# A graph-attention kernel: the next batch's load placed behind the store that frees its tile, its split and one batch's pieces reordered

## The chip, the cores and the metric

The kernel runs on one core of a Trainium2 chip. The core has a matrix engine (TensorE, in the profile PE, with PEld for its weight loads), three engines for element work (VectorE or DVE, ScalarE or ACT, GpSimd or POOL) and SyncE (SP), which here only starts transfers. The metric is the device time of one execution in microseconds, as the median of several runs. Before the change it is 4039.82 us (three runs, 4035.16 to 4045.39).

## The reference

The input x has 32 batches of 512 nodes with 512 features. Two layers follow each other, both with a residual and a normalisation over the features:

```python
# layer 0: messages along the graph
mi = einsum('bkd,od->bko', x, Wi)
mj = einsum('bkd,od->bko', x, Wj)
a = adj.astype(x.dtype)
deg = a.sum(axis=1)
out = deg[None, :, None] * (mi + b) + einsum('ij,bjo->bio', a, mj)
x = layernorm(x + out)
# layer 1: attention over the graph's edges, 8 heads of 64
q, k, v = x @ Wq.T + bq, x @ Wk.T + bk, x @ Wv.T + bv      # split in heads
scores = where(adj == 0, -inf, q @ k.T / 8)
x = layernorm(x + softmax(scores) @ v @ Wo.T + bo)
```

All batches use the same weights and the same adjacency matrix, and no batch depends on another.

## The kernel before, in words

**Pipeline over batches.** The work of the 32 batches is laid out in periods. In period n (`for n in range(1, B + 1)`, the loop around L695) TensorE does the attention of batch b = n - 1 in 8 steps: scores (L427), the product with the values (L448), the sums of the softmax (L455). Between these it does the dense products of three batches: `phase_b(n)` has layer 0 of batch n together with the output projection of m = n - 2; `phase_c(n)` has the v, q and k products of batch n; `phase_a(n + 1)` has the "gather" of batch n + 1 and what is left of k. Each phase returns a list of pieces in a fixed order with an estimated cost each (`PC, TR, GA = 1.73, 0.44, 1.9` us); `by_steps` cuts the list into 8 shares. The engines then run their instructions in just the order in which this list emits them: there is no scheduler behind it. An item of cost 0 (`z(...)`) is emitted where it stands.

**Pieces.** A product of 512x512 by 512x512 is cut into 2x2 blocks and done with seven block products instead of eight, numbered 1 to 7 and done in the order 1, 2, 6, 7, 4, 5, 3 (`ORDER`). `piece` (L359) does one of them: eight records of matmuls in a v, q, k or projection piece, sixteen in a layer 0 piece, since that has two products. Results are gathered in two PSUM banks, `mma` and `mmb`. Products 6, 7 and 4 add up in one bank, 5 and 3 in another (`GROUP`), so after 6 or 7 VectorE must have read the bank before the next of the group may go on in it.

**The gather of a batch.** `l0_gather` (L283) treats one quarter of x's features: four transposes on TensorE ("turning", L292), a product with the degrees on VectorE (L293), and eight matmuls with the adjacency matrix (L299) that use x split in a high and a low part. `split` (L178) makes these: ACT copies the high part `xhi` (L183), GpSimd subtracts to get the low part `xlo` (L184). `ahead` (L187) makes the first two of a batch's four splits; the others follow inside the gather.

**Tiles of x and their transfers.** A batch's x is 1 MB. There are three tiles for it, named `xh` (L106), and x is worked on in place until the batch is stored (L477). In period n, batch m = n - 2 is stored in `phase_c(n)`, right after its final normalisation (ACT, L272), and its tile takes x of batch n + 1 (`load_x`, L107), which the gather wants at the end of the same period. So a load must wait for the end of a store. SyncE starts all transfers in the order of the program, and it also starts the loads of the weight blocks: `prefetch` (L250) puts a new one into a ring of 12 tiles (L253) after each piece, when its TensorE work has freed one. An instruction of SyncE that waits holds back all that stand behind it.

**What the change touches.** In `phase_c`, the last items are the pairs of q and v pieces for products 6, 7, 4, 5, 3 (L600 to L603); `load_x(n + 1)` stands behind the pair of product 5 (L604, L605), and `ahead(n + 1)` behind all of them (L606, L607). In `phase_b`, the first period with n = 1 has no batch m yet, and its layer 0 pieces have an order of their own (L558), followed by the statistics of the first rows behind piece 4, the normalisation (`apply`), and two turnings of the normalised rows (`l0_norm`, L320).

Of the kernel before, what the change touches and what calls it, by code (L numbers as in the profile page):

```python
# [25 lines left out]
def gnn_attention_kernel(  # L26
# [35 lines left out]
    B, N, D = x.shape  # L62
# [266 lines left out]
    def quarter(src, j, n):  # L329
        return src[:, 2 * j:2 * j + 2, Q * n:Q * n + Q]  # L330
# [153 lines left out]
    def z(f, *a):  # L484
        return (0.0, f, *a)

    def pc(kind, b, i, bank):
        return (2 * PC if kind == "l0" else PC, piece, kind, b, i, bank)
# [4 lines left out]
    def banks(n):  # L493

        return ("a", "b") if n % 2 == 0 else ("b", "a")
# [46 lines left out]
    def project(m, i):  # L542

        res = [pc("pj", m, i, banks(m)[1])]
        if i == 1:
            res = [z(combos, TO, m, ot_quarter(m), (1,))] + res
        if i == 2:
            res = [FLUSH] + res + [z(combos, TO, m, ot_quarter(m), (2, 3, 4))]
        return res

    def phase_b(n):

        m = n - 2
        if m < 0:
            res = []
            side = [z(add_bo, 0, i) for i in range(2)]
            A, K = banks(n)
            for i, bank in ((2, A), (6, K), (5, A), (7, K), (3, A), (4, K)):  # L558
                res.append(pc("l0", n, i, bank))
                if i == 4:  # L560
                    res += [z(stats, n, 0)]
                res += side[:1]
                side = side[1:]
            return res + [z(apply, n, 0), z(stats, n, 1), (TR, l0_norm, n, 0), (TR, l0_norm, n, 1)]
        res = project(m, 1)
        for i in ORDER[1:]:
            res.append(pc("l0", n, i, banks(n)[0]))
            if i == 4:
                res.append(z(stats, n, 0))
            if i == 5:  # L570
                res.append(z(stats, m, 0))
            if i == 3:
                res += [z(stats, n, 1), (TR, l0_norm, n, 1)]
            res += project(m, i)
            if i == 4:
                res.append(z(apply, n, 0))
            if i == 5:
                res.append((TR, l0_norm, n, 0))
            if i in (7, 4):
                res.append(z(add_bo, n - 1, int(i == 4)))  # L580
        return res

    def phase_c(n):

        m = n - 2
        norm = [(TR, l0_norm, n, ic) for ic in range(NC)]
        h = lambda j, i: quarter(HT[n], j, i)
        A, K = banks(n)
        res = [pc("v", n, 1, A)] + ([z(apply, n, 1)] if n else []) + [pc("q", n, 1, K)]
        if m >= 0:  # L590
            res += [z(stats, m, 1)]
        res += [pc("v", n, 2, A), norm[2], norm[3], z(combos, TH, n, h, (1, 2)), pc("k", n, 1, A),
                z(combos, TH, n, h, (3, 4)), pc("q", n, 2, K), pc("k", n, 2, A)]
        side = []
        if n == 0:

            side = [z(graph_forms, 2), None, z(graph_forms, 0), None, z(graph_forms, 1)]
        if m >= 0:
            res += [z(apply, m, 0), z(apply, m, 1), z(store, m)]
        for i in ORDER[2:]:  # L600
            for f in pc("q", n, i, K), pc("v", n, i, A):
                res += [f] + [g for g in side[:1] if g]
                side = side[1:]  # L603
            if i == 5 and n + 1 < B:  # L604
                res += [z(load_x, n + 1)] if n > 0 else []  # L605
        if n + 1 < B:  # L606
            res += [z(ahead, n + 1)]  # L607
        return res

    def fold(part):  # L610
# [59 lines left out]
    def flags():  # L670
# [5 lines left out]
        nc.vector.tensor_scalar(again, tot, -1.0, 1.0, op0=OP.mult, op1=OP.add)  # L676

    PERIODS = [first() + phase_c(0) + phase_a(1)]
    PERIODS += [by_steps(phase_b(n) + phase_c(n) + phase_a(n + 1)) for n in range(1, B)]
    PERIODS += [last_steps()]  # L680
    for f in PERIODS[0] + [f for p in PERIODS[1:] for todo in p for f in todo]:
# [191 lines left out]
```

## Time and profile before

| what | value |
|---|---|
| time, median of 3 | 4039.82 us |
| span of the profiled execution | 4048.5 us |
| TensorE busy | 3902.1 us, 96% |
| VectorE / GpSimd / ScalarE busy | 2595.3 / 1862.8 / 1058.3 us |
| mean granted TensorE clock | 0.986 of full speed |
| loads of x, 1 MB each: start to landing | median 5.7 us |
| stores of x, 1 MB each: start to landing | median 5.2 us |

Three kinds of views are used. The table of waits gives, for an engine and a line, what it waited for: microseconds in total, times, longest. The timeline lists instructions with their start, their duration, engine and line, and in brackets how long the engine had been idle and what ended the idle time. A table of windows gives, for a stretch of the execution, each engine's busy time and number of instructions, and then the granted clock, the share of DMA and GB/s. A wait is put down to what came last; idle time of an engine that isn't the bottleneck costs nothing.

### The profile page before, as it was taken

How to read it: one execution, taken by the hardware profiler on the slowest of the kernel's cores; microseconds unless marked ns; L12 is line 12 of the kernel's file. 1: busy time of each engine (PE TensorE's matmuls, PEld its weight loads, DVE VectorE, ACT ScalarE, POOL GpSimd, SP SyncE). 2: the span in 40 equal slices, each digit the busy share in tenths (PEclk: the TensorE clock that was granted, in tenths of full speed). 3: DMA queues.
4: the chain of work that ended last, by engine and by line, in shares of the span. 5: the costliest groups of instructions: out<-in, count | busy, mean ns of one | idle time of the engine just before them, and what ended most of it. 6: DMA issues, size and time to landing. Idle time of an engine off the chain costs nothing.

```text
span 4048.5 us, 46895 instructions
## 1 busy us (share of the span) xinstructions
PE 3902.1 (96%) x17370; PEld 2663.9 (66%) x17370; DVE 2595.3 (64%) x3525; ACT 1058.3 (26%) x1476; POOL 1862.8 (46%) x1861
## 2 busy tenths in 40 slices
PE   9999999999999999999999999999999999999997
PEld 6666666666666666666666666666666666666663
DVE  4566665666666666666666666666666666666666
ACT  2222222222222222222223222222222222222322
POOL 4355444454434544345444445443454434544433
PEclk9999999999999999999999999999999999999998
DMA  7333333333334233333333433333423333333330
GB/s 247 107 104 97 110 99 115 107 98 104 110 106 123 84 112 102 108 117 92 104 110 104 117 105 100 103 107 110 122 81 111 106 110 114 104 97 110 102 110 22
DMA packets 281866, 433.86 MB, mean 107 GB/s; under 512 B 23073, under 2 KB 119841, under 8 KB 281633
## 3 DMA queue, kind: packets, MB, share of 16 engines
q1 hardware_dynamic: 281376, 430.27, 35.3%
q8 instruction: 141, 2.31, 0.2%
q14 instruction: 93, 0.75, 0.1%
q0 software_dynamic: 256, 0.53, 0.0%
HBM read 389.29 MB, written 41.42 MB: 106 GB/s over the span
## 4 chain that ended last, share of the span: by engine, by line
PE 72%; DVE 11%; POOL 9%; DMA 4%; issue 2%; ACT 1%; SPq 0%; POOLq 0%
PE mma L375 20%; PE mmb L375 20%; PE sc L427 10%; PE ov L448 9%; POOL xh L390 5%; DMA xh<-in_x_dram 4%; PE mmb L299 3%; PE mma L299 3%; DVE rl L461 3%; PE ov L455 2%; DVE st L265 2%; DVE xh L393 2%; POOL big L344 2%; DVE e L432 2%; POOL es L438 2%
## 5 line engine op out<-in xcount | busy, mean ns | idle before, releaser
L432 DVE TENSOR_TENSOR e<-sc,edge 128x1024 f32<-128x1024 f32 x512 | 602.4, 1218 | 467.3 <-ACT sc L431 467.3
L431 ACT ACTIVATE sc<-sc 128x1024 f32<-128x1024 f32 x512 | 492.9, 1007 | 1279.8 <-PE sc L427 1279.3
L375 PE MATMUL mmb<-ring,big 128*128 128x256 f32 x3144 | 734.6, 382 | 7.9 <-POOL big L344 7.9
L375 PE MATMUL mma<-ring,big 128*128 128x256 f32 x3112 | 724.2, 381 | 3.1 <-POOL big L344 2.9
L375 PEld LDWEIGHTS mmb<-ring,big 128*128 128x128 f32 x3144 | 593.2, 191 | 131.4 <-DVE e L432 23.5
L375 PEld LDWEIGHTS mma<-ring,big 128*128 128x128 f32 x3112 | 584.7, 190 | 125.4 <-DVE e L432 25.2
L344 POOL TENSOR_TENSOR big<-big 128x512 f32<-128x512 f32 x376 | 549.7, 1488 | 222.3 <-DVE big L293 177.9
L184 POOL TENSOR_TENSOR xlo<-xh,xhi 128x512 fp32r<-128x512 f32 x128 | 163.4, 1287 | 911.6 <-ACT xhi L183 909.4
L427 PE MATMUL sc<-q,k 64*128 64x512 f32 x2048 | 513.8, 620 | 0.0
L448 PE MATMUL ov<-e,v 128*64 128x512 f32 x2048 | 497.8, 607 | 8.2 <-DVE oT L471 8.2
L461 DVE RECIPROCAL rl<-ov 128x128 f32<-128x128 f32 x512 | 462.4, 929 | 5.6 <-PE ov L455 1.8
L375 PE MATMUL mma<-big,ring 128*128 128x256 f32 x1808 | 433.1, 382 | 2.2 <-DVE xh L393 2.2
L375 PE MATMUL mmb<-big,ring 128*128 128x256 f32 x1776 | 425.3, 382 | 3.2 <-DVE xh L393 2.4
L267 POOL TENSOR_SCALAR mv<-mv 128x1 f32<-128x1 f32 x256 | 50.3, 196 | 747.2 <-DVE mv L266 737.1
L375 PEld LDWEIGHTS mma<-big,ring 128*128 128x128 f32 x1808 | 337.9, 190 | 80.5 <-issue 26.0
L375 PEld LDWEIGHTS mmb<-big,ring 128*128 128x128 f32 x1776 | 332.2, 190 | 78.7 <-issue 24.3
L438 POOL TENSOR_TENSOR es<-e 128x1024 f32<-128x1024 f32 x128 | 300.7, 2349 | 176.5 <-PE ov L455 176.5
L448 PEld LDWEIGHTS ov<-e,v 128*64 128x64 f32 x2048 | 124.8, 136 | 349.0 <-issue 275.3
L440 DVE TENSOR_TENSOR es<-es,e 128x1024 f32<-128x1024 f32 x256 | 339.6, 1327 | 0.1
L427 PEld LDWEIGHTS sc<-q,k 64*128 64x128 f32 x2048 | 178.8, 189 | 214.4 <-issue 212.2
L393 DVE TENSOR_TENSOR xh<-xh,mmb 128x512 f32<-128x512 f32 x186 | 125.7, 676 | 217.4 <-PE mmb L375 216.4
L390 POOL TENSOR_TENSOR xh<-xh,p 128x512 f32<-128x512 f32 x186 | 231.7, 1274 | 72.4 <-ACT sc L431 39.0
(141 smaller groups left out, 3746.1 us busy)
## 6 DMA issues: line engine op xcount, KB each, us to landing
ring<-wq SPq DMA_DIRECT2D x160, 256.0 KB, 2.6
ring<-wv SPq DMA_DIRECT2D x160, 256.0 KB, 2.7
ring<-wk SPq DMA_DIRECT2D x160, 256.0 KB, 3.8
ring<-wi SPq DMA_DIRECT2D x155, 256.0 KB, 2.7
ring<-wj SPq DMA_DIRECT2D x155, 256.0 KB, 2.7
ring<-wo SPq DMA_DIRECT2D x155, 256.0 KB, 2.6
xh<-in_x_dram SPq DMA_DIRECT2D x32, 1024.0 KB, 5.7
out_dram<-xh SPq DMA_DIRECT2D x31, 1024.0 KB, 5.2
```

The source lines that it names most:

```text
L299: nc.tensor.matmul(pm, parts[w][:, jc, :], adjR[:, jc, :], start=(w == 0 and jc == 0), stop=(w == 1 and jc == NC - 1))
L344: nc.gpsimd.tensor_tensor(dst, p, q, op=OP.subtract)
L375: nc.tensor.matmul(pm[:, c * Q:(c + 1) * Q], lhs, rhs, start=first, stop=(kc == 1 and n == len(terms) - 1), skip_group_check=True)
L390: nc.gpsimd.tensor_tensor(d, d, p1, op=OP.add)
L393: nc.vector.tensor_tensor(d, d, pm, op=OP.add)
L427: nc.tensor.matmul(ps[:, s, :], KT[b, hp // 2][r, hp % 2, kc * P:(kc + 1) * P], QT[b, hp // 2][r, hp % 2, :], start=True, stop=True)
L431: nc.scalar.activation(ps, ps, AF.Exp, scale=QSCALE)
L432: nc.vector.tensor_tensor(e, ps, edge[:, kc:kc + 1, :].to_broadcast([P, 2, N]), op=OP.mult)
L438: nc.gpsimd.tensor_add(ES[hp], E[0], E[1])
L440: nc.vector.tensor_add(ES[hp], ES[hp], E[half])
L448: nc.tensor.matmul(PV[hp][s * HD:(s + 1) * HD, :], V[b][:, kc, c0:c0 + HD], E[kc][:, s, :], start=(kc == 0), stop=(kc == NC - 1))
L461: nc.vector.reciprocal(rl[:, c], pl[:, c])
```

## The change

Three edits of the order of the program; no instruction is added or taken away.

1. `load_x(n + 1)` moves from behind the q and v pieces of product 5 to behind those of product 7, four pieces earlier. The store of batch n - 2 stands ahead of the pieces of product 6, so the load comes close behind the store whose tile it takes.
2. `ahead(n + 1)`, the first two splits, moves from behind the pieces of product 3 to behind those of product 5, two pieces ahead of the turning.
3. In period 1, layer 0's piece 4 comes ahead of piece 3. The statistics of the first rows, which are emitted behind piece 4, come earlier with it.

The aim is that x of the next batch, and its split, are there when TensorE comes to turn it, and that in period 1 the normalised rows are there when TensorE turns them.

```diff
@@ phase_b(n), the period without a batch m
-            for i, bank in ((2, A), (6, K), (5, A), (7, K), (3, A), (4, K)):
+            for i, bank in ((2, A), (6, K), (5, A), (7, K), (4, K), (3, A)):
                 res.append(pc("l0", n, i, bank))
                 if i == 4:
                     res += [z(stats, n, 0)]
@@ phase_c(n)
             for f in pc("q", n, i, K), pc("v", n, i, A):
                 res += [f] + [g for g in side[:1] if g]
                 side = side[1:]
+            if i == 7 and 0 < n < B - 1:
+                res += [z(load_x, n + 1)]
             if i == 5 and n + 1 < B:
-                res += [z(load_x, n + 1)] if n > 0 else []
-        if n + 1 < B:
-            res += [z(ahead, n + 1)]
+                res += [z(ahead, n + 1)]
         return res
```

## The prediction

> **What bounds the kernel now.** I read the page's busy table first, then the waits of TensorE, then the timeline of one period, then windows with the granted clock. The busy table says which engine to look at:
>
> ```profile
> PE 3902.1 (96%) x17370; PEld 2663.9 (66%) x17370; DVE 2595.3 (64%) x3525; ACT 1058.3 (26%) x1476; POOL 1862.8 (46%) x1861
> ```
>
> TensorE (PE) is busy in 3902.1 of 4048.5 us; no other engine is over 64%. So only two things can shorten the run: less idle on PE (146.4 us), or faster matmuls. The waits of PE (total us, times, longest) say who owns the idle:
>
> ```profile
> PE sc L292 <- DMA xh<-in_x_dram: 89.3, 30, 5.5
> PE ov L448 <- DVE oT L471: 8.2, 4, 3.0
> PE mmb L375 <- POOL big L344: 7.9, 15, 5.0
> PE sc L320 <- ACT xh L272: 3.2, 2, 2.9
> ```
>
> One wait, 30 times, owns 89.3 us: the turning of the next x (L292) waits for the load of that x. Every other is under a tenth of it. The fourth line matters for the third edit. One period, from the store of an old batch to the scores behind the first gather, then the second gather for comparison (start, duration, engine, line; in brackets the idle before):
>
> ```profile
> 1292.78 0.39 SPq L477 DMA_DIRECT2D out_dram<-xh  x1
> ...
> 1296.05 0.50 SPq L253 DMA_DIRECT2D ring<-in_wjT_dram  x1
> 1297.73 0.34 SPq L253 DMA_DIRECT2D ring<-wk  x1
> ...
> 1307.37 0.41 SPq L107 DMA_DIRECT2D xh<-in_x_dram  x1
> ...
> 1308.43 1.89 PE L375 MATMUL mma<-ring,big 128*128 128x256 f32 x8
> ...
> 1312.74 1.14 ACT L183 CAST xhi<-xh 128x512 fp32r<-128x512 f32 x2 [12.01 <-DMA xh<-in_x_dram]
> ...
> 1312.76 0.66 PE L292 MATMUL sc<-ident,xh 128*128 128x128 f32 x4 [2.45 <-DMA xh<-in_x_dram]
> ...
> 1315.91 1.99 PE L427 MATMUL sc<-q,k 64*128 64x512 f32 x8
> ...
> 1322.38 0.60 PE L292 MATMUL sc<-ident,xh 128*128 128x128 f32 x4
> ...
> 1324.67 1.89 PE L375 MATMUL mma<-big,ring 128*128 128x256 f32 x8
> ```
>
> The load starts 14.59 us after the store that frees its tile, and its data comes 5.4 us later, when PE has already stopped. I measured the same distances in all 30 periods that load x in the loop. Start of the last piece to start of the turning: mean 4.87 us (4.17 to 7.38). Turning to the next work behind the first gather: mean 3.81 us (3.15 to 4.46). The second gather shows what these cost when nothing is waited for: 1322.38 to 1324.67 is 2.29 us, and a turning follows a piece by 1.72 us (1324.67 to 1326.39 in the same timeline). The clock explains why the block itself is slow:
>
> ```profile
> 1684.00:1694.00 10.00, 6.22 (x19) 4.06 (x19) 1.38 (x2) 2.24 (x4) 2.51 (x2) 0.66 0.38 140
> 1694.00:1808.00 114.00, 113.50 (x518) 78.11 (x515) 77.82 (x105) 30.72 (x42) 55.94 (x56) 1.00 0.34 100
> ```
>
> Sixth figure behind the window's length: granted clock. It is 0.66 in the ten microseconds around a stall and 1.00 in the 114 us of the same period that follow. So a stall costs its idle and a stretch of slow matmuls after it.
>
> **What the Trainium skill says.** "TensorE: Matmul & The Clock Gate", Part 1 and its section on HAM oscillation: the PE clock falls to half after an idle window of about 3.4 us and comes back after a busy one, and a loop that waits for a DMA each turn pays both every turn. The trace agrees: stalls of 2.3 to 5.5 us, dips to 0.66, some periods with the fast block of 3.15 us (the window fell elsewhere) and most near 4. "DMA: Bandwidth & Descriptors", Anatomy of one DMA: a semaphore wait is made on the issuing sequencer, not in the DMA engines. So a load that waits for a store holds back whatever SyncE has queued behind it. The trace before shows that kind of blocking at the store: SPq L477 waits for ACT L272 163.8 us over 31 stores, 5.3 us each, without a PE wait on any ring tile. Same page, Measured: 1 MB from HBM takes 6.15 us; the trace has 5.7 us median for this load, which I use.
>
> **The change part by part.**
>
> *The load four pieces up.* On SyncE it now stands behind the load of 1296.05, ahead of that of 1297.73. The tile is free when the store has landed: 1292.78 + 5.2 (median landing of the store; 4.2 to 5.4) = 1298.0, and SyncE is there by 1296.6. So the load issues near 1298.2 instead of 1307.37, 9.2 us sooner. It adds a wait of some 1.6 us on SyncE. Behind it stand only ring loads, and the first of them was issued at 1297.73 before, so it slips by under 1 us. The ring is 12 tiles deep: the first ring load after the wait serves a piece more than 30 us later (the load at 1282.53 is for the piece at 1320.55). The wait is hidden by that depth; cost nothing. Arrival: with the median 5.7 us, 1303.9. From below: 5.2 us, the shortest landing, gives 1303.4. From above: 8.4 us (the slowest in the loop, 558.44 to 566.86), and before it four ring loads of 256 KB, issued while the store runs, which is another 1 MB in the queue: about 1 MB in the 5.2 us of the store, less its completion, so some 3.3 us (estimate); 1298.2 + 8.4 + 3.3 = 1309.9. PE wants x at 1308.43 + 1.72 = 1310.15. I take 1305: in time, five microseconds to spare, and at the worst bound just in time, with part of the split still to come.
>
> *The split after it.* ACT's two copies last 0.62 us each and GpSimd's subtraction 1.27 us, so the first piece is split 1.9 us after arrival: 1306.9 in my value, and its second half is wanted at 1310.15 + 0.36 + 1.01 = 1311.5. ACT is idle from 1300.74 to 1312.74 and GpSimd waited 23.85 us before its first one, so nothing stands in front.
>
> *The split's place in the program.* It moves ahead of the q and v pieces of product 3. These have only TensorE and VectorE work (the result is added by VectorE), so the instruction order of ACT and of GpSimd is the same as before in every period. It removes and adds nothing: 0 us. If a reader expects the "two pieces ahead" to bring time by itself, this is where I disagree; what moves the split is x.
>
> *Gain of the two.* A period loses 4.87 - 1.72 = 3.15 us ahead of the turning and 3.81 - 2.29 = 1.52 us in the block. The rest of the period (from the next work to the last piece before the next stall) is 116.00 us in the mean and 115.85 at its shortest; that 0.15 is the slow clock's tail. Sum 4.82 us, times 30 = 145 us. This is about what the pair of 89.3 us of wait and a mean clock of 0.986 (at most 1.4% of 4048.5 = 57 us) allow: 146. Everything downstream (VectorE, GpSimd combinations at L344) hangs on the turning itself and moves with it.
>
> *Batch 1's pieces.* Before, after piece 4 come scores, then PE waits 2.86 us for the normalised rows (L320 at 143.58, where L455 at 139.69 plus 0.96 would give 140.65) and the slow clock stretches L320, L320, L375 to 4.63 us where about 2.6 is normal: 4.9 us lost, once. After, piece 4 follows piece 7 in the same bank, so it must wait until VectorE has added piece 7's result: the addition starts 0.2 us after the piece ends and lasts 0.69 us, so about 1.0 us of idle. In return piece 3 (3.5 us) lies between piece 4 and the scores, and statistics and ACT's normalising finish while the scores run. Net 4.9 - 1.0 = 3.9 us gained; bounds 0 (the wait for the rows stays) and 4.9. Queued behind the waiting piece: only piece 3 and the scores, moved by that 1 us.
>
> Sum: 145 + 4 = 149 us of the profiled execution, 4048.5 - 149 = 3899.5. The unprofiled median is 8.7 us shorter than the profiled span. Periods differ only in stall and clock, so that difference may be stall, which is then not there to be won twice (3899), or overhead of the base (4039.8 - 149 = 3891). I take 3897.
>
> **The rivals.**
> (1) The load arrives late in part: the queued ring loads and the store's tail push it to 1309 or later, and the wait becomes one for the split (ACT L183, POOL L184). For it: DMA runs at 205 GB/s in this stretch, and one landing of 8.4 us. Against it: the five spare microseconds. Half the gain: 4040 - 73 = 3967.
> (2) The stall moves: another wait just behind becomes the bound (VectorE, or L344's combinations of GpSimd with 7.9 us now). For it: PE would be 99% busy, every small wait shows. Against it: VectorE, ACT and GpSimd are idle for 2, 12 and 24 us ahead of the first gather. If 2 us a period came back: 4040 - 89 = 3951.
> (3) Slower: SyncE, held by the wait for the store, starves the ring, or a PE without rests loses clock. Against it: more than 30 us of ring depth, and 114 us at clock 1.00. A loss of 1 us a period without the gain: 4070.
>
> **How the numbers follow.** Forecast 0.84, (1) 0.07, (2) 0.05, (3) 0.02, no change (the wait of L292 is a consequence of something I misread) 0.02. Predicted 3897. Range: the bottom is the lower of the two sums, 3891, less 0.3% for how runs of one kernel differ (4035.2 to 4045.4 before), 3880; the top leaves 3.2 us of stall a period in ten periods and batch 1's gain at 0, 3897 + 32 + 4, and some of (2): 3940. Faster 0.95, same 0.02, slower 0.03.
>
> **What would show it.** The row PE L292 <- DMA xh gone or under 10 us; x loads about 5.4 us after their stores; mean clock 0.995 or more; periods of about 119.9 us instead of 124.6; ACT's wait at L183 for the DMA down from 12 us a period to some 3 to 5; PE L320 <- ACT gone, and a wait of about 1 us of PE L375 for DVE L393 once. I would be wrong if L292 or L299 still waits for x, xhi or xlo, or if ring tiles appear among PE's waits.

## The result and the profile after

The changed kernel takes 3907.32 us (median of 4 runs, 3905.9 to 3908.04), the kernel before 4041.39 us in the same comparison. The ratio is 0.9669, with a 95% interval of 0.9652 to 0.9686: 134 us less, 3.3%. The profiled execution has a span of 3904.1 us (4048.5 before) and a mean granted clock of 0.997 (0.986). The busy table after:

```profile
PE 3848.6 (99%) x17370; PEld 2639.9 (68%) x17370; DVE 2606.6 (67%) x3525; ACT 1057.8 (27%) x1476; POOL 1900.3 (49%) x1861
```

TensorE has the same 17370 matmuls, and yet its busy time fell by 53.5 us. Busy time isn't work: part of it was matmuls that ran on a slow clock or stood waiting with the engine counted as busy. Its idle time fell from 146.4 to 55.5 us. The first of TensorE's waits, and the row (2.2 us before) that holds the one wait which the third edit adds:

```profile
PE ov L448 <- DVE oT L471: 8.2, 4, 3.0
PE mmb L375 <- POOL big L344: 7.9, 15, 5.0
...
PE mma L375 <- DVE xh L393: 3.0, 15, 0.8
```

The wait of L292 for x (89.3 us) is gone, and no ring tile has come in. On SyncE, the load now waits for the store:

```profile
SPq L477 <- ACT xh L272: 161.3, 31, 60.7
...
SPq L107 <- DMA out_dram<-xh: 42.0, 29, 1.9
```

That is 1.4 us in each of 29 periods. (The store's own wait for ACT is as before. Of the 161.3 us one store has 60.7 and the other 30 have 3.4 each in the mean; the prediction's "5.3 us each" spreads such an outlier, 63.2 us, over all.) One period of the timeline after, to be read beside that of before:

```profile
1245.55 0.39 SPq L477 DMA_DIRECT2D out_dram<-xh  x1
...
1250.85 0.37 SPq L107 DMA_DIRECT2D xh<-in_x_dram  x1
1251.31 1.51 SPq L253 DMA_DIRECT2D ring<-wk  x1
...
1257.55 1.14 ACT L183 CAST xhi<-xh 128x512 fp32r<-128x512 f32 x2 [4.05 <-DMA xh<-in_x_dram]
...
1258.24 3.48 POOL L184 TENSOR_TENSOR xlo<-xh,xhi 128x512 fp32r<-128x512 f32 x2 [15.90 <-ACT xhi L183]
...
1261.25 1.99 PE L375 MATMUL mma<-ring,big 128*128 128x256 f32 x8
...
1263.08 0.60 PE L292 MATMUL sc<-ident,xh 128*128 128x128 f32 x4
...
1265.45 1.99 PE L427 MATMUL sc<-q,k 64*128 64x512 f32 x8
```

The load starts 5.3 us after its store (14.6 before), x is there 12.0 us after it, and TensorE turns it 17.5 us after it: 5.5 us to spare, and at least 4.7 in every period. The turning follows the last piece by 1.83 us and the block to the scores lasts 2.37 us, with nothing waited for. Over the 30 periods that load x in the loop: last piece to turning 1.77 us (4.87 before), block 2.37 us (3.81); from load to load, the first left out, 120.07 us (124.64).

### The profile page after: what moved, and what is told of

Same layout as the page of the kernel before. It is cut to its first block, busy times and chain, and to the rows that moved or that the text cites. A ratio compares the mean times of both kernels' runs of the same rounds, so it can differ in the third digit from the quotient of the medians.

```text
span 3904.1 us, 46897 instructions
## 1 busy us (share of the span) xinstructions
PE 3848.6 (99%) x17370; PEld 2639.9 (68%) x17370; DVE 2606.6 (67%) x3525; ACT 1057.8 (27%) x1476; POOL 1900.3 (49%) x1861
## 4 chain that ended last, share of the span: by engine, by line
PE 76%; DVE 12%; POOL 9%; issue 2%; ACT 1%; DMA 0%; SPq 0%; POOLq 0%
PE mma L375 22%; PE mmb L375 22%; PE sc L427 10%; PE ov L448 9%; POOL xh L390 5%; PE mmb L299 3%; DVE rl L461 3%; PE mma L299 3%; PE ov L455 2%; DVE st L265 2%; DVE xh L393 2%; POOL big L344 2%; DVE e L432 2%; POOL es L438 2%; PE sc L292 2%
## 5 line engine op out<-in xcount | busy, mean ns | idle before, releaser
L184 POOL TENSOR_TENSOR xlo<-xh,xhi 128x512 fp32r<-128x512 f32 x128 | 200.6, 1577 | 738.2 <-ACT xhi L183 738.2
L440 DVE TENSOR_TENSOR es<-es,e 128x1024 f32<-128x1024 f32 x256 | 353.4, 1380 | 0.1
```

What stands on the lines that cost most here:

```text
L440: nc.vector.tensor_add(ES[hp], ES[hp], E[half])
```

## The experiments

**The three edits, each taken out of the changed kernel.**

Without the third (batch 1's order):

```diff
-            for i, bank in ((2, A), (6, K), (5, A), (7, K), (4, K), (3, A)):
+            for i, bank in ((2, A), (6, K), (5, A), (7, K), (3, A), (4, K)):
```

> The changed kernel without its third edit: batch 1's pieces stand as before (3 ahead of 4). My theory, the load is nearly all: about 3.4 us slower than the changed kernel's 3907.3, so 3910.7, with TensorE's wait of about 2.9 us at L320 for ACT back. Rival, the reordering sets period 1's rhythm for all that follow: a loss of tens of us, 3940 or more.

Measured 3910.66 us, 3.3 us slower than the changed kernel, and 3.0 us slower than the kernel of the next experiment, which ran beside it. The wait is back as it was:

```profile
PE sc L320 <- ACT xh L272: 3.5, 2, 2.9
```

Without the second (the split's place):

```diff
-            if i == 5 and n + 1 < B:
-                res += [z(ahead, n + 1)]
+        if n + 1 < B:
+            res += [z(ahead, n + 1)]
```

> The changed kernel without its second edit: the first two splits are emitted behind product 3's pieces again. My theory: the instruction order and the waits of every engine are the same as in the changed kernel, so 3907 within 2 us. Rival, the split's place is what hides the split: its 1.9 us a period come back in part, 3930 to 3960.

Measured 3907.71 us against 3907.32. The instructions of every engine, their order and their waits are those of the changed kernel; only the numbers in tile names differ. The second edit changes the text of the program and nothing else.

Without the first (the load's place):

```diff
-            if i == 7 and 0 < n < B - 1:
+            if i == 5 and 0 < n < B - 1:
                 res += [z(load_x, n + 1)]
```

> The changed kernel without its first edit: the load stands behind product 5's pieces as before, with the splits right behind it and batch 1's new order. My theory: 4041 less about 3.4 us, so 4037, with the 89 us of waits of L292 for the DMA as before. Rival, splits emitted early gain by themselves: 3960 to 4010.

Measured 4039.91 us, beside 4044.85 for the kernel before: ratio 0.9993 (0.9984 to 1.0002). The wait of L292 is back with 83.3 us. So the first edit is the gain, but for some 3 us of the third (which this run alone could not tell from nothing).

**How early is early enough.** The load behind product 4's pieces, between the two places:

```diff
-            if i == 7 and 0 < n < B - 1:
+            if i == 4 and 0 < n < B - 1:
```

> The changed kernel with the load two pieces later, behind product 4's pieces: it issues some 5.5 us later than in the changed kernel, and there x arrives 5.5 us before it is wanted. My theory: the gain is a threshold, x before the turning or not. x then arrives about when it is wanted, its split a little late: 3907 to 3935. Rival, the gain is in proportion to how early the load is: half of it, about 3970.

Measured 3911.51 us: all of the gain but 4 us. In the period at 1245 the load starts 11.13 us after its store, so of the 9.3 us by which the change moves it, 5.8 are given up, and x comes 0.7 us before it is turned. So the gain is not in proportion to how early the load is: it is nearly all there once x comes before the turning. This kernel also has the cleanest view of the block behind a turning whose x is only just there:

```profile
1502.87 1.14 ACT L183 CAST xhi<-xh 128x512 fp32r<-128x512 f32 x2 [9.64 <-DMA xh<-in_x_dram]
...
1502.89 0.66 PE L292 MATMUL sc<-ident,xh 128*128 128x128 f32 x4
1503.55 0.75 PEld L299 LDWEIGHTS mmb<-adjR,xhi 128*128 128x128 f32 x4 [0.24 <-ACT xhi L183]
...
1504.92 0.77 PEld L299 LDWEIGHTS mmb<-adjR,xlo 128*128 128x128 f32 x4 [0.62 <-POOL xlo L184]
...
1506.06 1.99 PE L427 MATMUL sc<-q,k 64*128 64x512 f32 x8
```

TensorE stood idle for 0.1 to 0.2 us only, and its granted clock is 1.00 from 1500 to 1508; the block still lasts 3.17 us instead of 2.37, because ACT and GpSimd split x while TensorE waits for the halves. That is also the fast block of the kernel before (3.15 us).

**Idle time and slow clock.** In the kernel before, TensorE was given work that is thrown away ahead of the first turning of each loaded batch; x stays as late as it was. The turnings of the identity land where the real ones then write.

```diff
         pt = turn_tile()
+        if adjT is None and dc == 0 and b > 1:
+            for _ in range(16):
+                nc.tensor.transpose(pt[:, 0:P], ident, ident)
```

> The kernel before, with 16 turnings of the identity ahead of the first turning of each loaded batch, overwritten by the real one: 16 x 0.15 = 2.4 us of TensorE work that is thrown away, in the place of the shortest stall. x arrives as late as before. My theory, a stall costs its idle and then half-clock matmuls: the idle stays lost (as filler), the block behind it goes from 3.81 to 2.38 us and the slow tail goes, 30 x 1.5 = 45 us, so 3996. Rival, the slow clock is only another view of the idle: 4041, or above it where the filler delays the turning.

Measured 4028.43 us; ratio 0.9956 (0.994 to 0.9973), some 18 us where I had 45. Sixteen turnings took 1.9 us, not 2.4, so 35.7 us of waits for x were left, and five blocks still had 3.87 to 4.03 us. With 28 of them (3.2 us):

> The filler kernel with 28 turnings instead of 16; one took 0.12 us, so 3.3 us of filler. It is meant to part the slow clock from the late split in the block behind the stall. If what is left of the block's excess is the split, which starts only when x is there: no dips of the clock, block between 2.4 and 3.15 us and never 4, time 4020 to 4035 since the filler now delays some turnings. If it is still the clock: blocks of 4 us stay.

Measured 4021.98 us; ratio 0.9942 (0.9923 to 0.996). Only 7.2 us of waits for x are left and the granted clock is 0.996. No block is longer than 3.16 us; the eight whose turning still waited for x are at 3.15 or 3.16, the others, whose turning the filler held up while the split went on, at 2.56 to 3.15. A period in which x came with the end of the filler (L293 is the filler, L295 the turning and L302 the gather here):

```profile
3531.67 3.22 PE L293 MATMUL sc<-ident 128*128 128x128 f32 x28
3535.05 0.66 PE L295 MATMUL sc<-ident,xh 128*128 128x128 f32 x4 [0.16 <-DMA xh<-in_x_dram]
3535.70 1.21 PE L302 MATMUL mmb<-adjR,xhi 128*128 128x512 f32 x4
3537.07 1.20 PE L302 MATMUL mmb<-adjR,xlo 128*128 128x512 f32 x4 [0.16 <-POOL xlo L184]
```

And a period of the kernel before, after a stall of 2.67 us:

```profile
1436.33 0.66 PE L292 MATMUL sc<-ident,xh 128*128 128x128 f32 x4 [2.67 <-DMA xh<-in_x_dram]
1436.98 1.69 PE L299 MATMUL mma<-adjR,xhi 128*128 128x512 f32 x4
1438.47 1.95 PE L299 MATMUL mma<-adjR,xlo 128*128 128x512 f32 x4
1440.35 2.22 PE L427 MATMUL sc<-q,k 64*128 64x512 f32 x8
```

```profile
1437.40:1440.90 3.50, 3.50 (x10) 2.12 (x10) 0.32 (x1) 0.50 (x2) 2.12 (x2) 0.51 0.02 5
```

The last line is a window in this period: its granted clock is 0.51. The second half (L299 with `xlo`) falls in it and lasts 1.95 us instead of 1.20, stretched by the clock; the first half (with `xhi`), 1.69 us, has the wait for the split and the beginning of the slow stretch in it.

The clock records of that trace say more. The granted clock is 1 or one half, nothing between (the 0.66 of the prediction is the mean of a window). Of the 30 stalls 22 are followed or overlapped by a stretch of half clock, of 3.41 us or twice that, and they are just those with a block over 3.2 us. The length of the stall does not decide it alone: one of 2.29 us had such a stretch, one of 2.92 us had none. All stretches of the trace begin on one grid of 3.41 us. In the grid's window ahead of each of the 22, TensorE is busy for at most 1.70 us; of the windows around the stalls that have full clock and none of these stretches behind them, all but three are busy for 1.81 us or more. In the kernel before with a ring of 4 tiles (used below) the two figures are 1.72 and 1.81, without exception. So it seems to count how much of one window of the grid a stall takes, about half being enough; no run moved a stall along the grid to test it.

So a stall in the kernel before has three parts, counted in this order. Idle: 4.87 - 1.77 = 3.10 us. Late split: 3.15 - 2.37 = 0.78 us. Slow clock: 3.81 - 3.15 = 0.66 us in the block, and 0.08 us behind it (the rest of the period is 116.00 us before and 115.92 after). Together 4.62 us, times 30 = 139 us of the profiled execution. The clock's share, 30 x 0.74 = 22 us, fits what the 28 turnings saved, 23 us (16 to 31 by the ratio's interval), but only roughly, since they also held some turnings up.

**Does SyncE's wait cost anything, and what hides it.** The load directly behind the store:

```diff
             res += [z(apply, m, 0), z(apply, m, 1), z(store, m)]
+        if 0 < n < B - 1:
+            res += [z(load_x, n + 1)]
...
-            if i == 7 and 0 < n < B - 1:
-                res += [z(load_x, n + 1)]
```

> The changed kernel with the load directly behind the store on SyncE, which then waits the whole 5.2 us for the store with four ring loads behind it. My theory, the ring of 12 tiles hides this: 3907 within 3 us, no ring tile among TensorE's waits. Rival, SyncE held back starves the pieces: slower by 1 to 5 us a period, 3940 to 4060.

Measured 3909.54 us, 2 us from the changed kernel, though the wait for the store is now 112.1 us in total, 3.9 each. Nor does it help: in the period at 1244 the load starts 4.24 us behind the store instead of 5.30. It can, since a store behind which no load of the ring is started lands sooner: 4.3 us in the median, not 5.2. Then the ring was cut to four tiles (`RING = 4` for `RING = 12`), in the changed kernel, in this one, and in the kernel before as their control.

> The changed kernel with a ring of 4 tiles instead of 12. If the ring's depth is what makes the wait for the store harmless, a load issued behind x lands some 6 to 7 us later and its piece comes about 7 us later: waits of TensorE of 0 to 2 us a period for ring tiles, 3907 to 3970. If the depth is not needed, 3907.

> Load directly behind the store and a ring of 4 tiles. If depth hides SyncE's wait, this is where it shows: four loads held 5.2 us and then queued behind 1 MB of x, TensorE waits 4 to 8 us a period for ring tiles and the clock falls: 4030 to 4150. If depth plays no part, as with 12 tiles, 3907.

> The kernel before with a ring of 4 tiles: the control to the changed kernel with 4, which lost all its gain to a wait of 2.8 us a period for the first ring tile issued behind the store. If that wait belongs to the store (SyncE held by ACT ahead of it, and 1 MB in front), it is here too and comes on top of the stall for x: 4041 + 130 = 4170, ratio of the pair near 0.967 again. If it belongs to the moved load, this kernel has it not: about 4041.

| load of x stands | ring of 12 | ring of 4 | TensorE's wait for a ring tile with 4 |
|---|---|---|---|
| behind product 5 (before) | 4040 to 4045 us | 4135.54 us | 82.4 us |
| behind product 7 (changed) | 3907.32 us | 4036.42 us | 82.3 us |
| directly behind the store | 3909.54 us | 4190.22 us | 218.1 us |

The rows behind the last column, of the changed kernel with 4 tiles, and then of the kernel with the load at the store:

```profile
PE mmb L375 <- DMA ring<-wq: 41.8, 15, 2.8
PE mma L375 <- DMA ring<-wq: 40.5, 15, 2.8
```

```profile
PE mmb L375 <- DMA ring<-wq: 111.1, 15, 8.2
PE mma L375 <- DMA ring<-wq: 107.0, 15, 8.1
```

With 4 tiles the changed kernel loses 129 us, more than the range that I had, and with the load at the store 4190 us is above its range too. The control says whose wait that is: the kernel before has it to a tenth of a microsecond, 2.7 us a period for the first weights behind the store. It belongs to the store, which holds SyncE until ACT has normalised the rows and then puts 1 MB in front of the next tile (which of the two it needs was not tested); the moved load adds nothing to it. Directly behind the store it does: the timeline of that kernel has the load, then the ring's tile, and then TensorE:

```profile
1325.05 0.39 SPq L477 DMA_DIRECT2D out_dram<-xh  x1
...
1329.32 0.38 SPq L107 DMA_DIRECT2D xh<-in_x_dram  x1
1329.80 0.46 SPq L253 DMA_DIRECT2D ring<-wq  x1
...
1335.48 3.75 PE L375 MATMUL mmb<-big,ring 128*128 128x256 f32 x8 [7.23 <-DMA ring<-wq]
```

The first tile is asked for 4.75 us after the store instead of 0.5, and comes behind x. So the depth of the ring does hide SyncE's wait for the store, and the four loads between store and x keep the moved load from adding to it where the depth is small; with 4 tiles the first edit is still worth 99 us. I had 4170 for the control; it lost 93 us to the ring rather than 130. Its stall for x was smaller (75.4 us of waits) and its blocks shorter (3.45 us), and the slow clock took different shares (mean clock 0.988 here, 0.984 in the changed kernel with 4 tiles). Why the two kernels lose 93 and 129 us with the same wait was not followed further.

## Why the prediction was right, and where its terms were off

*Which wait.* Right: the wait of L292 for x went from 89.3 us to none, and with the load put back it is 83.3 us.

*When x comes.* The load was put at 5.4 us behind the store and is at 5.3. Its arrival was put at 12.2 us behind the store and is at 12.0 in the period shown; the landing takes 6.6 us in the median instead of 5.7. With the load at the store, ahead of the ring's loads, it is 5.7 again; so the loads in front seem to cost some 0.9 us, where the prediction's upper bound had 3.3, an estimate whose part for the completion no trace here shows. (The 6.15 us of the Trainium skill's "DMA: Bandwidth & Descriptors", Measured, are for transfers that GpSimd issues; here SyncE does, and the trace decides.) Five microseconds to spare were foreseen, 5.5 are there.

*The split's place costs and brings nothing.* Right, 3907.71 against 3907.32.

*SyncE's wait.* "Some 1.6 us", hidden by the ring: 1.4 us, no ring tile among the waits. Shown by taking the depth away.

*The block.* Here a step was wrong, in its cause: "The clock explains why the block itself is slow". Of the 1.44 us by which the block was too long, 0.78 are the split that starts only when x is there, which the trace of before would have shown, and 0.66 the clock. In the very period that the prediction shows, the block lasts 3.15 us at a granted clock of 1.00 (the window at the end), and the weight loads of L299 wait 0.23 us for ACT's half and 0.60 for GpSimd's:

```profile
1313.41 0.77 PEld L299 LDWEIGHTS mmb<-adjR,xhi 128*128 128x128 f32 x4 [0.23 <-ACT xhi L183]
...
1314.78 0.76 PEld L299 LDWEIGHTS mmb<-adjR,xlo 128*128 128x128 f32 x4 [0.60 <-POOL xlo L184]
```

```profile
1310.30:1316.00 5.70, 3.08 (x15) 1.86 (x14) 1.38 (x2) 1.14 (x2) 2.54 (x2) 1.00 0.55 206
```

The sum did not suffer, since an early x cures both; that is luck in this step. The wrong cause did show in the expectation of the filler, 45 us for what measured 18.

*The sum.* 149 us of the profiled execution were forecast; the spans differ by 144.4. The terms that were too large: the block ends at 2.37 and not 2.29 us, since scores follow it and not a piece (30 x 0.08 = 2.4 us); the turning follows by 1.77 and not 1.72 (1.5 us); the clock's tail gives 0.08 and not 0.15 us (2 us); batch 1's order 3.3 and not 3.9 us. They come to 6.5 us where 4.6 are missing; the 2 us that came in elsewhere were not traced. The rest of the way from 3897 to 3907 is the base. The prediction took the 8.7 us between profiled span and median half as overhead of the profile. But an execution's time is longer than its span, by 1.8 us (3905.9 against 3904.1), and the profiled execution of before took 4050.38 us, 10.6 more than the median. Its excess went with the stalls, as the close times after (3905.9 to 3908.04) suggest, and the 3899.5 reckoned from the span was the better number.

*Batch 1.* Its wait for the bank is there, 0.78 us where 1.0 was put, and the turned rows no longer wait for ACT:

```profile
128.41 3.72 PE L375 MATMUL mma<-ring,big 128*128 128x256 f32 x16 [0.78 <-DVE xh L393]
```

*The rivals.* A load late in part (1) came only with the load moved back behind product 4, and then cost 4 us. A stall that moves (2) did not come: the rest of the period is as long as before. Starvation or a slower clock (3): only with a ring of 4.

The Trainium skill's clock gate ("TensorE: Matmul & The Clock Gate", HAM oscillation) describes in the main what was found: stalls of about 3 us in each turn of the loop, half clock with 22 of 30 of them, and a clock near 1 once the idle is filled, be it with work that is thrown away. In one point the trace does not agree, though the prediction said so: the page asks for an idle window of about 3.4 us, and 15 of the 22 stalls were shorter, down to 2.29 us; about half of a window was enough. The clock's cost here, 0.74 of 4.62 us a period, is the smaller part.

## What to carry to other kernels

When a load waits for the store that frees its buffer, ask for the distance between the two in the timeline: 14.6 us between instructions that could stand 5.3 us apart, ahead of a consumer that stalled for 3, were some 131 us of 4041 for one moved line (the other 3 are batch 1's order). Put it early enough and no earlier: between store and load leave the transfers that others wait for, since the wait is made by the queue that issues them. With 12 tiles of lookahead that made no difference here, with 4 it made 154 us. And price a stall with what hangs behind it, the conversion that can't start and the clock: 4.6 us for 3.1 us of idle.

## What had not been expected of the hardware

GpSimd's two subtractions of a first split took 2.54 us together in the kernel before:

```profile
1313.44 2.54 POOL L184 TENSOR_TENSOR xlo<-xh,xhi 128x512 fp32r<-128x512 f32 x2 [23.85 <-ACT xhi L183]
```

In the changed kernel they fall beside VectorE's addition at L440 and took 3.48 us in the period shown (1258.24) and 4.29 in the next (1377.20), while that addition, 1.22 us otherwise, took 1.86 and 1.51 us. Over the whole execution a subtraction went from 1.29 to 1.58 us in the mean. Moving work earlier can make it slower. The prediction had the 1.27 us of before for it; the difference is hidden by the 5 us to spare. Whether the two slow each other, or something else slows both, was not tested.
